# A perceiver block on one core: bias rows turned in 32 by 32 squares, the output bias added later, a longer stretch of written order, and a shorter E4M3 rounding

## The chip, the cores and the metric

The kernel is one launch on one NeuronCore of a Trainium2 chip. Its time is the device time of that core in microseconds (us), from launch to the end of the program. The core's engines each follow their own instruction stream: TensorE (PE in the profile, with its weight loads shown as PEld), VectorE (DVE), ScalarE (ACT), GpSimd (POOL) and SyncE (SP), which here only issues DMAs. They meet through semaphores.

## The reference

Eight batches of 128 rows and 512 features go through three layers; each adds to its input.

```python
x = x + xattn(layernorm(x), ctx, Wq, Wk, Wv, Wo, bo)        # 8 heads of 64, 2048 context rows of 384
x = x + attn(layernorm(x), Wq, bq, Wk, bk, Wv, bv)          # one head of 512, causal mask, softmax over
                                                            # axis 1 of the logits; adds its input twice
x = x + ffn(layernorm(x), w1, b1, w2, b2)                   # 512 -> 2048 -> 512

def ffn(x, w1, b1, w2, b2):
    h  = relu(einsum('bsd,hd->bsh', x, w1) + b1)
    hq = float_quantize(h, 4, 3)      # 4 exponent bits, 3 of mantissa, subnormals, overflow to inf
    wq = float_quantize(w2, 4, 3)
    out = einsum('bsh,dh->bsd', hq, wq) + float_quantize(b2, 5, 10)
    return float_quantize(out, 5, 10)
```

In the second layer the logits are (x Wq + bq)(x Wk + bk)^T. The kernel multiplies Wq and Wk into one matrix and needs the biases only as three small things: bq times bk (one number), Wq times bk (512 numbers, a bias of the keys) and Wk times bq (512 numbers, a row that each x is multiplied with). The key bias is called `side`, the row `u`.

## The kernel before

**Stages.** A head (0 to about 92 us) loads, computes all queries, and the keys and values of batch 0. Then eight batches of cross attention follow. Each has four steps m (two heads each): `scores(b, m)` on TensorE, VectorE reading the eight score banks (L530), ScalarE's exponentials (`exps`, L544), transposes of 32 by 32 squares on VectorE (`turns`, L557), 16 DMAs that move the squares to their places, and one step later `attend` (L571). Between them lie pieces of the next keys and values (`k_proj` L427, `v_proj` L450), which are done by a block product that needs sums of the inputs (`sum_half` L205 for the context, `sum_w` L226 to L239 for the weights). In the last batch these pieces are replaced by the beginning of the self attention of rows 0 to 3: at m = 1 the joint weight (`both_weights`, psw L664), then the four rows' norms (`normed_into` L111 to L118, the product with `u` L649, the bias L652) and their transposes (`turn`, pt_s L131), at m = 2 the keys (psk L678). The feed-forward layer closes (ph L927, pf L936).

**Orders.** TensorE runs in program order throughout. `in_turn` (L241) holds ScalarE and `first` (L243) holds VectorE in program order; both are closed at L859 and L860, in step m = 0 of the last batch. After that, and on POOL and SP everywhere, a scheduler chooses the order from its own estimate of times when the program is built; on the chip each engine then runs strictly in the chosen order.

**The bias rows.** `sa_bk` and `sa_bq` come as 128 columns of 4 numbers. `across` (L284) writes them, 4 bytes at a time, to a line of 512 numbers in DRAM; a second DMA reads that line into all 128 partitions (`row_bk`, `row_bq`, L297). All these DMAs are on POOL's queue. `dot` (L302) multiplies two tiles on VectorE and sums over the row. `dot(both_biases, ...)` and `weight_by_bias(0)` (four dots) stand ahead of `k_proj(0, 0, (1,))` in program order (L783 to L785), `weight_by_bias(1)` behind it. `turn_weight` (L310) transposes squares of Wq and Wk on VectorE; `keep_weights` (L315) writes them out with 32 DMAs on SP.

**The output bias.** `bo` is loaded into all partitions (L276). `keep_rows` (L501) adds it to the eight rows of x on POOL and writes them to DRAM (`xd`) on SP, before `load_q(0)` in program order. `bo`, `row_bk` and `row_bq` share two buffers (tag "t", `TMPB` = 2). The rows `x_in` lie in the buffer that the first transposed exponentials (`pT`) will need.

**Rounding.** `quantize` (L28) rounds with five VectorE instructions: mask the exponent, clamp it, add and subtract a multiple of it (two scalar_tensor_tensor), and scale up and down so that overflow becomes infinite. `quantize_w2` uses it on 16 chunks of w2 (128x512), `hidden` on blocks of four hidden chunks (128x1024; two chunks, 128x512, in the last two blocks), `finish` with the wider format on the result.

Of the kernel before, what the change touches and what calls it, by code (L numbers as in the profile page):

```python
# [17 lines left out]
P = 128  # L18
# [4 lines left out]

E4M3 = (3, -6, 8)
E5M10 = (10, -14, 16)


def quantize(nc, pool, out, x, fmt, tag):  # L28

    man, least, over = fmt
    shape = list(x.shape)
    e = pool.tile(shape, F32, tag=f"{tag}_e", name=f"{tag}_e")
    r = pool.tile(shape, F32, tag=f"{tag}_r", name=f"{tag}_r")
    magic = 1.5 * 2.0 ** (23 - man)
# [4 lines left out]
    nc.vector.tensor_scalar(out, r, 2.0 ** (128 - over), 2.0 ** (over - 128), ALU.mult, ALU.mult)  # L44


@with_exitstack
def tile_perceiver_block(
# [225 lines left out]
    nc.sync.dma_start(wv, xa_wv.rearrange("(k p) n -> p k n", p=P))  # L274
    bo = tmp.tile([P, D], F32, tag="t", name="bo")
    nc.sync.dma_start(bo, xa_bo.partition_broadcast(P))  # L276


    w_sa = vp.tile([P, 2, NK, D], F32, tag="v1", name="w_sa")
    side = const.tile([P, 2, NK], F32, tag="side", name="side")  # L280
# [24 lines left out]
    def weight_by_bias(i):  # L305

        for k in range(NK):
            dot(side[:, i, k : k + 1], w_sa[:, i, k], bias_rows[i])

# [190 lines left out]

    def keep_rows(g):  # L501
        for b in range(g * GB, (g + 1) * GB):
            nc.gpsimd.tensor_tensor(xs[b], xs[b], bo, ALU.add)
        nc.sync.dma_start(xd[:, ts(g, GB), :], x_in[:, ts(g, GB), :])
# [129 lines left out]
    class SelfAttention:  # L634
# [37 lines left out]
        def keys(self, both):  # L672

            self.kt = self.pool.tile([P, NK, GT], F32, tag="sk", name=f"sk_{self.g}")
            for m in range(NK):
                ps = bank(f"psk_{self.g}_{m}")
                for k in range(NK):
                    nc.tensor.matmul(  # L678
                        ps, both[:, k, ts(m, P)], self.xt[:, k, :],
                        start=(k == 0), stop=(k == NK - 1),  # L680
                    )
                nc.scalar.activation(
                    self.kt[:, m, :], ps, AF.Identity, bias=side[:, 0, m : m + 1]
                )
                if m == 1:
                    yield
# [116 lines left out]
    for b in range(B):  # L803
        last = b + 1 == B
        for m in range(NK):
# [45 lines left out]
            if m == 0:  # L851
# [39 lines left out]
    b2r = load_row(wff, b2, "b2r")  # L891
    b1c = load_columns(wff, b1, "b1c")
    w2 = wff.tile([P, NHC, D], BF16, tag="w2", name="w2")
# [17 lines left out]
    def hidden(batches, xt, blocks):  # L911
# [117 lines left out]
```

## Time and profile before

Three runs took 1124.47, 1125.67 and 1127.59 us; the median is 1125.67 us. The profiled execution took 1124.47 us, of which 1122.7 us lie between its first and its last instruction (its span).

| engine | busy us | share of the span | instructions |
|---|---|---|---|
| PE | 1098.4 | 98% | 6254 |
| PEld | 830.2 | 74% | 6254 |
| DVE | 844.1 | 75% | 1760 |
| ACT | 334.7 | 30% | 527 |
| POOL | 236.1 | 21% | 328 |

How to read it: times within the execution count from the span's start. A line of a timeline gives start, duration (of the whole group where it says xN), engine, line of the kernel, operation, output<-input and shapes. A chain line gives start, duration and what ran. In a table of waits, "A <- B: total, times, longest" means that A stood still until B was done. The granted clock is TensorE's clock as the throttle allowed it, 1.00 being full speed.

### The profile page before, as it was taken

How to read it: one execution, taken by the hardware profiler on the slowest of the kernel's cores; microseconds unless marked ns; L12 is line 12 of the kernel's file. 1: busy time of each engine (PE TensorE's matmuls, PEld its weight loads, DVE VectorE, ACT ScalarE, POOL GpSimd, SP SyncE). 2: the span in 40 equal slices, each digit the busy share in tenths (PEclk: the TensorE clock that was granted, in tenths of full speed). 3: DMA queues.
4: the chain of work that ended last, by engine and by line, in shares of the span. 5: the costliest groups of instructions: out<-in, count | busy, mean ns of one | idle time of the engine just before them, and what ended most of it. 6: DMA issues, size and time to landing. Idle time of an engine off the chain costs nothing.

```text
span 1122.7 us, 16820 instructions
## 1 busy us (share of the span) xinstructions
PE 1098.4 (98%) x6254; PEld 830.2 (74%) x6254; DVE 844.1 (75%) x1760; ACT 334.7 (30%) x527; POOL 236.1 (21%) x328
## 2 busy tenths in 40 slices
PE   9989999999999999999999999999998999999997
PEld 4467788877878887888778788878874564687775
DVE  3988767767867786677777667866787468997777
ACT  3323232222223332322222233323232323232221
POOL 1401610440053045004400530350002100000001
PEclk9989999999999999999999999999998999999999
DMA  8858544553553355445535533554474445200001
GB/s 213 279 129 135 129 99 111 146 151 76 142 143 83 85 148 146 101 109 146 150 76 142 141 76 85 148 137 92 108 209 120 108 95 225 75 1 20 10 10 38
DMA packets 66785, 130.10 MB, mean 116 GB/s; under 512 B 27456, under 2 KB 32592, under 8 KB 65808
## 3 DMA queue, kind: packets, MB, share of 16 engines
q1 hardware_dynamic: 64144, 121.68, 43.6%
q0 software_dynamic: 1696, 6.57, 2.0%
q8 instruction: 49, 0.80, 0.3%
q10 hardware_dynamic: 864, 0.79, 0.2%
q14 instruction: 32, 0.26, 0.1%
HBM read 51.92 MB, written 9.97 MB: 55 GB/s over the span
## 4 chain that ended last, share of the span: by engine, by line
PE 88%; DVE 7%; DMA 3%; issue 1%; ACT 0%; SPq 0%; ACTq 0%; DVEq 0%
PE pv_z L450 20%; PE pk_z L427 19%; PE po L571 11%; PE sc L526 10%; PE ph L927 9%; PE pv_b L450 3%; PE pk_b L427 3%; PE psk L678 2%; PE psv L717 2%; PE py L609 2%; PE pf L936 2%; DMA x<-in_ctx_t_dram 1%; PE psw L664 1%; DVE m L205 1%; DMA x_in<-in_x_dram 1%; DVE x L205 1%
## 5 line engine op out<-in xcount | busy, mean ns | idle before, releaser
L544 ACT ACTIVATE p<-p,nm 128x2048 f32<-128x2048 f32 x64 | 128.2, 2003 | 429.4 <-DVE nm L538 291.2
L557 DVE STREAM_TRANSPOSE p<-p 128x512 f32<-128x512 f32 x256 | 158.9, 680 | 82.8 <-ACT p L544 82.6
L530 DVE TENSOR_SCALAR_CACHE_REDUCE p<-sc 128x512 f32<-128x512 f32 x256 | 159.0, 686 | 21.0 <-PE sc L526 18.6
L450 PE MATMUL pv_z<-wv_sums,x 128*128 128x256 f32 x640 | 158.0, 381 | 1.8 <-DVE v L353 1.8
L427 PE MATMUL pk_z<-x,wk_sums 128*128 128x256 f32 x600 | 151.0, 385 | 5.5 <-DVE kt L353 4.9
L205 POOL TENSOR_TENSOR m<-x 128x256 f32<-128x256 f32 x70 | 51.1, 731 | 485.4 <-DMA x<-in_ctx_t_dram 388.9
L450 PEld LDWEIGHTS pv_z<-wv_sums,x 128*128 128x128 f32 x640 | 120.4, 190 | 20.3 <-DVE v L353 2.2
L427 PEld LDWEIGHTS pk_z<-x,wk_sums 128*128 128x128 f32 x600 | 113.4, 191 | 25.1 <-DVE kt L353 5.6
L571 PEld LDWEIGHTS po<-pT,v 128*64 128x64 f32 x2048 | 112.4, 138 | 25.0 <-issue 23.5
L526 PE MATMUL sc<-kt,q 64*128 64x512 f32 x512 | 120.9, 604 | 3.8 <-DVE p L530 2.5
L571 PE MATMUL po<-pT,v 128*64 128x128 f32 x2048 | 120.2, 276 | 0.0
L927 PE MATMUL ph<-xf,w 128*128 128x256 f32 x512 | 111.3, 379 | 0.0
L450 PE MATMUL pv_z<-wv_sums,m 128*128 128x256 f32 x448 | 107.5, 380 | 0.2 <-ACT v L347 0.2
L927 PEld LDWEIGHTS ph<-xf,w 128*128 128x128 f32 x512 | 97.2, 190 | 13.9 <-issue 0.5
L427 PE MATMUL pk_z<-m,wk_sums 128*128 128x256 f32 x420 | 102.0, 381 | 0.0
L526 PEld LDWEIGHTS sc<-kt,q 64*128 64x128 f32 x512 | 47.6, 187 | 63.7 <-issue 52.7
L450 PEld LDWEIGHTS pv_z<-wv_sums,m 128*128 128x128 f32 x448 | 83.3, 190 | 13.3 <-issue 0.9
L427 PEld LDWEIGHTS pk_z<-m,wk_sums 128*128 128x128 f32 x420 | 79.8, 191 | 11.7
L347 ACT COPY v<-pv_z 128x512 f32<-128x512 f32 x112 | 62.8, 588 | 59.8 <-PE pv_z L450 59.6
L347 ACT COPY kt<-pk_z 128x512 f32<-128x512 f32 (+1 forms) x112 | 59.7, 558 | 63.1 <-PE pk_z L427 62.7
L205 POOL TENSOR_TENSOR x<-x 128x256 f32<-128x256 f32 x98 | 69.9, 730 | 0.8 <-DMA x<-in_ctx_t_dram 0.7
L350 DVE TENSOR_TENSOR v<-pv_z,v 128x512 f32<-128x512 f32 x96 | 63.2, 686 | 5.1 <-PE pv_z L450 5.0
(187 smaller groups left out, 1233.1 us busy)
## 6 DMA issues: line engine op xcount, KB each, us to landing
pT<-p SPq DMA_DIRECT2D x512, 128.0 KB, 2.4
x<-in_ctx_t_dram SPq DMA_DIRECT2D x45, 512.0 KB, 5.6
w<-in_w_t_dram SPq DMA_DIRECT2D x1, 4096.0 KB, 12.6
w2f<-in_w_t_dram SPq DMA_DIRECT2D x16, 256.0 KB, 2.7
x_in<-in_x_dram SPq DMA_DIRECT2D x8, 256.0 KB, 13.0
xd<-x_in SPq DMA_DIRECT2D x2, 1024.0 KB, 4.4
qd<-xq SPq DMA_DIRECT2D x8, 256.0 KB, 5.2
q<-qd SPq DMA_DIRECT2D x8, 256.0 KB, 3.1
```

The lines of the kernel that those rows point to most:

```text
L205: eng.tensor_tensor(x_block(b, h, to), x_block(b, h, one), x_block(b, h, two), ALU.add if op == "+" else ALU.subtract,)
L347: nc.scalar.copy(outs[ij], views(ps))
L350: nc.vector.tensor_tensor(outs[to], views(ps), outs[other], op)
L427: nc.tensor.matmul(ps[:, ts(i, BK)], wk_sums[:, WSLOT[WAT[r]], f2, :], x_block(b, h, XAT[r]), start=start and i == 0, stop=True, skip_grou ...
L450: nc.tensor.matmul(ps[:, ts(t, 256)], x[:, ts(t, P)], wv_sums[:, WSLOT[WAT[r]], :], start=start and t == 0, stop=True, skip_group_check=True,)
L526: nc.tensor.matmul(pair[i], q[r, :], kts[b, m // 2][r, m % 2, ts(n, 512)], start=True, stop=True)
L530: nc.vector.tensor_scalar(p[:, :, i].rearrange("p g (t i) -> p t g i", i=SQ)[:, ts(n, Q)], pair[i].rearrange("p (t g i) -> p t g i", g=Q, ...
L544: nc.scalar.activation(p[:, :, i], p[:, :, i], AF.Exp, bias=nms[b, m][:, i : i + 1], scale=SCALE, accum_out=sums[b][:, h : h + 1],)
L557: nc.vector.transpose(p[:, g, i], p[:, g, i])
L571: nc.tensor.matmul(pos[b][h * DH : (h + 1) * DH, ts(m, P)].rearrange("p (a i) -> p a i", a=Q), v[:, jt % 8, ts(2 * m + h, DH)], turned_[b, ...
L609: nc.tensor.matmul(ps, ot[:, ts(k, P)], wo[:, k, :], start=(k == 0), stop=(k == NK - 1))
L927: nc.tensor.matmul(ps[:, :n], w1[:, k, ts(c, P)], xt[:, k, at], start=(k == 0), stop=(k == NK - 1),)
```

## The change

Four edits.

1. **Bias rows by squares.** `sa_bk` and `sa_bq` are now loaded on SP (behind the loads of Wq and Wk) into the first four columns of zeroed 128x32 tiles (`squares`). `across(n)` transposes one such tile on VectorE in squares of 32, so that each band of 32 partitions holds four rows of 32 numbers, and writes them to DRAM with four POOL DMAs of four 128-byte pieces each. `spread_biases()`, called after the two `sum_half` of VectorE and before `sum_w` of the values' weights, does this for both rows and reads them back into all partitions. The third line, `u`, goes the same way behind `weight_by_bias(1)`.
2. **Output bias.** `bo` is allocated and loaded behind `weight_by_bias(0)`, in the buffer that `row_bk` leaves, and `keep_rows` follows it. The whole `turn_weight(0)` moves there too, ahead of `k_proj(0, 0, (1,))`.
3. **Program order.** `first` and `in_turn` are closed at the end of step m = 1 of the last batch, behind the norms and transposes of rows 0 to 3, and no longer at the end of m = 0.
4. **Rounding to E4M3.** `round_e4m3` gets x and a second tile c, which ScalarE makes: |x| (or relu of the same sum) times 2^20 in bfloat16. Subtracting x from c in float32 rounds it to the last place of c, three binary places below the leading one of x. VectorE clamps c, subtracts x from it, subtracts the difference from c, and scales: four instructions, two of them on bfloat16 alone. ScalarE gets one more activation for each chunk. The wider format keeps `quantize`.

```diff
-E4M3 = (3, -6, 8)
...
+UP = 2.0**20
+LOWEST, HIGHEST = 1.5 * 2.0**14, 2.0**30
+INFINITE = 2.0**120
+def round_e4m3(nc, pool, out, x, c, tag):
+    d = pool.tile(list(x.shape), F32, tag=f"{tag}_d", name=f"{tag}_d")
+    nc.vector.tensor_scalar(c, c, LOWEST, HIGHEST, ALU.max, ALU.min)
+    nc.vector.tensor_tensor(d, c, x, ALU.subtract)
+    nc.vector.tensor_tensor(out, c, d, ALU.subtract)
+    nc.vector.tensor_scalar(out, out, INFINITE, 1.0 / INFINITE, ALU.mult, ALU.mult)
...
-    bo = tmp.tile([P, D], F32, tag="t", name="bo")
-    nc.sync.dma_start(bo, xa_bo.partition_broadcast(P))
...
-    def across(v, n, name):
-        line = dram.tile([1, D], F32, tag=f"line{n}", name=f"line_{n}")
-        nc.gpsimd.dma_start(line.rearrange("o (k p) -> p (o k)", p=P), v)
-        return line[0].partition_broadcast(P)
+    squares = const.tile([P, 3, SQ], F32, tag="squares", name="squares")
+    nc.gpsimd.memset(squares, 0.0)
+    def across(n):
+        line = dram.tile([NK, P], F32, tag=f"line{n}", name=f"line_{n}")
+        nc.vector.transpose(squares[:, n], squares[:, n])
+        for a in range(Q):
+            nc.gpsimd.dma_start(line[:, ts(a, SQ)], squares[a * SQ : a * SQ + NK, n])
+        return line.rearrange("k p -> (k p)").partition_broadcast(P)
...
+    for n, a in enumerate((sa_bk, sa_bq)):
+        nc.sync.dma_start(squares[:, n, :NK], a)
     bias_rows = []
-    for n, a in (("bk", sa_bk), ("bq", sa_bq)):
-        c = const.tile([P, NK], F32, tag=f"c{n}", name=f"c_{n}")
-        nc.gpsimd.dma_start(c, a)
-        t = tmp.tile([P, D], F32, tag="t", name=f"row_{n}")
-        nc.gpsimd.dma_start(t, across(c, n, n))
-        bias_rows.append(t)
+    def spread_biases():
+        for n in range(2):
+            t = tmp.tile([P, D], F32, tag="t", name=f"row_{n}")
+            nc.gpsimd.dma_start(t, across(n))
+            bias_rows.append(t)
...
     sum_half(0, 1, nc.vector)
     sum_half(0, 0, nc.vector)
+    spread_biases()
     sum_w(lambda k, j: wv3[:, k, j, :], wv_sums, nc.vector)
     q_proj(1, both[1], qds[1], range(NK))
-    for g in range(NG):
-        keep_rows(g)
     load_q(0)
     dot(both_biases, bias_rows[0], bias_rows[1])
     weight_by_bias(0)
+    bo = tmp.tile([P, D], F32, tag="t", name="bo")
+    nc.sync.dma_start(bo, xa_bo.partition_broadcast(P))
+    for g in range(NG):
+        keep_rows(g)
+    turn_weight(0, range(NK))
     all_of(k_proj(0, 0, (1,)))
     weight_by_bias(1)
-    u_line = across(side[:, 1], "u", "u")
-    turn_weight(0, range(2))
+    u_line = across(2)
     values = first_of(v_proj(0, 0))
     first_of(values)
-    turn_weight(0, range(2, NK))
     turn_weight(1, range(NK))
     keep_weights()
...
                 if last:
-                    first.close()
-                    in_turn.close()
                     sap, w = enter_self_attention()
                     sa0 = SelfAttention(0, sap, w)
             if last and m == 1:
                 for r in sa0.rows:
                     sa0.norm(r)
                     sa0.turn(r)
+                first.close()
+                in_turn.close()
...
-            quantize(nc, tp, w2[:, c, :], w, E4M3, "qb")
+            up = tp.tile([P, D], BF16, tag="w2c", name=f"w2c_{c}")
+            nc.scalar.activation(up, w, AF.Abs, scale=UP)
+            round_e4m3(nc, tp, w2[:, c, :], w, up, "qw")
...
+            up = tp.tile([P, per, n], BF16, tag="hc", name=f"hc_{b0}_{c0}")
...
                 nc.scalar.activation(h[:, i, :], ps[:, :n], AF.Relu, bias=b1c[:, c : c + 1])
-            quantize(nc, tp, firsts[b0][:, c0 : c0 + per, :], h, E4M3, "qh")
+                nc.scalar.activation(
+                    up[:, i, :], ps[:, :n], AF.Relu, bias=b1up[:, c : c + 1], scale=UP
+                )
+            round_e4m3(nc, tp, firsts[b0][:, c0 : c0 + per, :], h, up, "qh")
```

More of the change, by code (lines that the diff above doesn't have):

```diff
@@ L274, in tile_perceiver_block @@
     nc.sync.dma_start(wv, xa_wv.rearrange("(k p) n -> p k n", p=P))
-    bo = tmp.tile([P, D], F32, tag="t", name="bo")
-    nc.sync.dma_start(bo, xa_bo.partition_broadcast(P))
     w_sa = vp.tile([P, 2, NK, D], F32, tag="v1", name="w_sa")
-    side = const.tile([P, 2, NK], F32, tag="side", name="side")
+    side = const.tile([P, NK], F32, tag="side", name="side")
     both_biases = const.tile([P, 1], F32, tag="both_biases", name="both_biases")
     turned_w = [dram.tile([D, D], F32, tag=f"tw{i}", name=f"tw_{i}") for i in range(2)]
-    def across(v, n, name):
-        line = dram.tile([1, D], F32, tag=f"line{n}", name=f"line_{n}")
-        nc.gpsimd.dma_start(line.rearrange("o (k p) -> p (o k)", p=P), v)
-        return line[0].partition_broadcast(P)
+    squares = const.tile([P, 3, SQ], F32, tag="squares", name="squares")
[6 more added lines that the diff above has]
+        return line.rearrange("k p -> (k p)").partition_broadcast(P)
     for i, a in enumerate((sa_wq, sa_wk)):
         nc.sync.dma_start(w_sa[:, i], a.rearrange("(k p) n -> p k n", p=P))
+    for n, a in enumerate((sa_bk, sa_bq)):
+        nc.sync.dma_start(squares[:, n, :NK], a)
     bias_rows = []
-    for n, a in (("bk", sa_bk), ("bq", sa_bq)):
-        c = const.tile([P, NK], F32, tag=f"c{n}", name=f"c_{n}")
-        nc.gpsimd.dma_start(c, a)
-        t = tmp.tile([P, D], F32, tag="t", name=f"row_{n}")
-        nc.gpsimd.dma_start(t, across(c, n, n))
-        bias_rows.append(t)
+    def spread_biases():
[3 more added lines that the diff above has]
+            bias_rows.append(t)
     unread = ps_acc.tile([P, D], F32, tag="po", name="unread")
@@ L307, in weight_by_bias @@
         for k in range(NK):
-            dot(side[:, i, k : k + 1], w_sa[:, i, k], bias_rows[i])
+            to = squares[:, 2] if i else side
+            dot(to[:, k : k + 1], w_sa[:, i, k], bias_rows[i])
     def turn_weight(i, ks):
@@ L682, in keys @@
                 nc.scalar.activation(
-                    self.kt[:, m, :], ps, AF.Identity, bias=side[:, 0, m : m + 1]
+                    self.kt[:, m, :], ps, AF.Identity, bias=side[:, m : m + 1]
                 )
@@ L892, in tile_perceiver_block @@
     b1c = load_columns(wff, b1, "b1c")
+    b1up = wff.tile([P, NHC], F32, tag="b1up", name="b1up")
+    nc.gpsimd.tensor_scalar(b1up, b1c, UP, None, ALU.mult)
     w2 = wff.tile([P, NHC, D], BF16, tag="w2", name="w2")
```

## The prediction

> **What bounds the kernel now.** First the page: TensorE is busy for 98% of the span. A change pays only where TensorE stands still, or where it makes it stand still.
>
> ```profile
> PE 1098.4 (98%) x6254; PEld 830.2 (74%) x6254; DVE 844.1 (75%) x1760; ACT 334.7 (30%) x527; POOL 236.1 (21%) x328
> ```
>
> Second, TensorE's own waits, here those near the edits.
>
> ```profile
> PE pk_z L427 <- DVE kt L353: 4.9, 1, 4.9
> PE sc L526 <- DVE p L530: 2.5, 1, 2.5
> ...
> PE sc L526 <- DVE rows L612: 1.3, 1, 1.3
> ...
> PE pf L936 <- DVE hq L44: 0.5, 1, 0.5
> ```
>
> The 4.9 us lie in the head (62.97 to 67.90), the 2.5 and 1.3 us in the last batch around 850, the 0.5 us near the end.
>
> Third, the timelines of VectorE and POOL in the head. While POOL adds bo (38.16 to 49.6), a sum of 128x256 takes VectorE 1.37 us; before and after, 0.42 (0.36 from start to start).
>
> ```profile
> 38.16 0.42 DVE L205 TENSOR_TENSOR m<-x,m 128x256 f32<-128x256 f32 x1
> 38.62 1.37 DVE L205 TENSOR_TENSOR x<-x 128x256 f32<-128x256 f32 x1
> ...
> 49.78 0.41 DVE L205 TENSOR_TENSOR x<-x,m 128x256 f32<-128x256 f32 x1
> ...
> 63.65 0.69 DVE L303 SCALAR_TENSOR_TENSOR unread<-row_bk,row_bq 128x512 f32<-128x512 f32 x1
> ...
> 67.43 0.41 DVE L353 TENSOR_TENSOR kt<-kt,pk_z 128x256 f32<-128x256 f32 x1
> ```
>
> ```profile
> 38.16 11.41 POOL L503 TENSOR_TENSOR x_in<-x_in,bo 128x512 f32<-128x512 f32 x8 [19.88 <-DVE m L205]
> ```
>
> Fourth, the windows: after each of the two long stops TensorE's granted clock (behind its five engines, before the DMA share) is 0.50 for 6.83 us.
>
> ```profile
> 66.31:73.14 6.83, 5.24 (x12) 4.21 (x13) 4.26 (x12) 0.37 (x1) 0.00 (x0) 0.50 0.35 130
> ...
> 851.38:858.20 6.82, 4.72 (x28) 3.22 (x30) 6.79 (x23) 1.06 (x1) 0.00 (x0) 0.50 0.01 4
> ```
>
> Fifth, the chain in the last batch, where `attend` takes 4.95 us at the halved clock and 3.65 elsewhere, and one VectorE line of a norm that met a POOL addition.
>
> ```profile
> 853.48 2.07 PE sc L526 x2
> 855.55 4.95 PE po L571 x64
> 860.50 13.93 PE psw L664 x32
> 874.43 1.75 PE pt_s L131 x16
> 876.18 3.63 PE sc L526 x16
> ```
>
> ```profile
> 936.44 1.77 DVE L649 SCALAR_TENSOR_TENSOR unread<-xn_s,u 128x512 bf16<-128x512 f32 x1
> ```
>
> **The head (edits 1 and 2).** Moving `keep_rows` away frees eight slowed sums: from 38.62 to 49.78 they take 11.16 us, at 0.36 each they would take 2.9. The sums end at 58.48 - 8.3 = 50.2, `sum_w` (13 instructions, 5.2 us) at about 55.6. POOL loses the old bias DMAs of the first 18 us; they may let the context land up to 1 us earlier, which I leave out.
>
> But the rows now start late. The transposes of 128x32 end at about 50.4 (a 128x512 one takes 0.68). POOL issues a DMA in 0.54 to 0.79 us, so the eight of the two lines take 4.4 to 6.1. How long four pieces of 128 bytes take to land no row shows. The nearest is the write of turned weights (the same 128-byte pieces, SP's queue), 2.1 us; the column load b1c on POOL's queue took 3.2, and the old line of 512 pieces of 4 bytes 9.9. I take 2.1 to 3.2, by the piece size, and keep 9.9 for a rival. The read into 128 partitions: b2r, same form and queue, 3.5 us when all was quiet, row_bq 6.0 under traffic. With both lines ahead of both reads the second line has landed at 54.25 + 2.1 to 3.2 = 56.4 to 57.5 and the second row at 60 to 63.5; with the first read between the lines (POOL would stand behind its wait) at 62 to 67. So the dots start at 60 to 67, middle 63.5, against 63.65 now: the 8.3 us are eaten by the row's way through DRAM. Behind them stand five dots (0.79 each, 3.9) and the four transposes of `turn_weight(0)` (0.61 each, 2.5, new there), then L353, for which TensorE waits. It goes on at 66.7 to 73.8, middle about 70.1 instead of 67.90. Of the extra 2.2 us some returns: the clock is halved until 73.14 anyway, and what starts later spends less in it: 5.2 us at half rate become 3.0. Net +1.5, with ends -2 (rows at 60) and +5.
>
> What is queued behind. `bo` waits on SP for the last dot of `weight_by_bias(0)` (about 67.6), lands 4 to 9 us later (b2r 3.5, bo 8.7), and POOL's eight additions (11.4) lie between 72 and 88. There they slow the four dots of `weight_by_bias(1)`, from 0.79 to about 1.4 each (one per addition), 2.6 us; VectorE has 2.5 us of transposes less in that stretch, and `v_proj` needs its first VectorE result only at its eleventh product, 3 us after it had it. Cost 0. On SP the two writes of xd (waiting for POOL), the two loads behind them and the 32 writes of turned weights (79.15 to 101.6, 0.7 us each) share one queue. If the scheduler puts the first weights ahead of xd, the queue ends near 102 as now; the turned weights leave the buffer that `v_proj(0, 1)` first writes at 107.55. About 5 us of cover; x_in leaves pT's buffer by 96, which is first written at 109. Cost 0. u's line is read only at 843. Nothing else of the head waits.
>
> **The last batch (edit 3).** Gained: L612 and the score readings (L530) no longer stand behind norms. From 845.70 TensorE needs 3.63 (scores) + 3.65 (attend) and starts psw at 852.98, not 860.50: -7.5, of which 1.3 is the clock. psw ends at 866.9.
>
> Lost: the norms now follow the whole step in both orders. ScalarE's order is exp, two psw copies, exp, two psw copies, load of the Sqrt table, then per row square root and copy. The last psw copy ends at 867.45, the table load (1.28) at 868.73; square root 0.29, reciprocal 0.16, normalize 0.54 with their gaps: first row at 869.85. TensorE, which had 1.75 us of transposes here without a wait, now stands. Each further row costs one round on VectorE: product with u 0.69, its sum and bias 0.15, statistics 0.60 and 0.15, square root 0.35, reciprocal 0.2, normalize 0.55: 2.7 us (the row's transpose and copy, 1.2, fit beside the first half). But POOL adds the row to x (1.27 us) just behind each normalize. Of the eight products with u, the one that met this took 1.77. Then a round is 3.75. The fourth row is ready at 869.85 + 3 x 2.7 to 3.75 = 878 to 881.1, the next scores start at 878.5 to 881.6 instead of 876.18: +2.3 to +5.4. In 867 to 881 TensorE works only 0.44 us per round, so I expect the halved clock again, as at 851; if it holds to about 883.9, it takes 2.7 or 1.1 us more. I take the round of 3.75, since the products that took 0.69 had no addition behind them: +5.4 + 1.1, rounded down to +6; ends +2.3 and +8.
>
> The Trainium skill (SBUF — State Buffer, Who interferes with whom) says that any VectorE instruction with two SBUF inputs is blocked for the whole of a GpSimd instruction that reads SBUF. By it the one-column bias addition L652 waits even where the product slips in first, so 3.75 is the only round; by the seven fast products alone it would be 2.7, and the total 3 us lower before the clock. No row shows L652 against an addition.
>
> Later TensorE is continuous until 931, so this shift stays. The norms of rows 4 to 6 are now placed by the scheduler behind 881; if ahead of score readings, up to 4 us more.
>
> **The rounding (edit 4).** Between 974.56 and 1100.65 TensorE is busy throughout (126.09 of 126.09 us in the windows), so fewer VectorE instructions give nothing there, and ScalarE's second activation (0.47 of each 1.73 us) hides too: ScalarE has 1.25 us free per chunk. If a chunk of w2 held ScalarE's queue, seven PSUM banks cover 12 us. Only the tail counts: the last chain of five (0.42, 0.43, 0.69, 0.69, 0.43; ends 1111.03) becomes one activation (0.47, to 1108.52) and four: two bfloat16 ones between 0.2 and 0.43, two of 0.69. End 1110.4 to 1110.8: -0.4, and the result's chain moves with it.
>
> **Sum.** +1.5 + 6 - 0.4 = +7.1 on the profiled execution's 1124.47 us: 1131.6, 5.9 above the median of 1125.67. I say 1131.5.
>
> **The rivals.** *The norms hide (faster).* The last batch keeps its 7.5 us if the rows come faster than TensorE needs them; break-even is a fourth row at 875.6, a round of 1.9 us. For it: the old norms finished unseen. Against: the round's own rows add to 2.7 on two engines in strict order. Full price: 1124.47 + 1.5 - 7.5 - 0.4 = 1118. Chance 0.15.
> *The two parts cancel.* Round of 2.7, full clock, head -2: 1124.47 - 2 + 2.3 - 0.4 = 1124.4; with the head at 0, 1126.4. Chance 0.17.
> *The lines land as slowly as before* (9.9, then a read of 7.5, as u took): second row at 54.25 + 9.9 + 0.5 + 7.5 = 72.2, TensorE at 79.1, +11 instead of +1.5: 1141. For it: the same queue; against: 16 pieces in place of 512. Chance 0.08.
> *SP's queue blocks*: xd ahead of all turned weights; they start at 88, end at 111, and `v_proj(0, 1)` waits 3 to 4 us: 1135. Chance 0.1.
> *My forecast*, 0.5, own range 1128 to 1135.
>
> **Range and chances.** 1119 to 1139 reaches from the hidden norms to a half-slow line; about 0.1 lies beyond each end. A measurement here tells 0.3% (3.4 us) from no change. Slower: forecast 0.5 less 0.03 for its low end, lines 0.08, queue 0.1, together 0.65. Same: the cancelling case and low end less 0.03 that falls below, 0.17. Faster: hidden norms and that 0.03, 0.18.
>
> **What would show it.** Head: sums at 0.36 us apart to 50; L303's first dot led by a wait for row_bq; TensorE's wait for L353 still 4 to 10 us. Last batch: no wait of sc for L612, psw at 853, then a wait of pt_s for xn_s of 9 to 13 us in four pieces and a clock of 0.50 around it. Tail: no wait for the last rounding above 0.2. I am wrong if pt_s hardly waits (the orders don't bind as I read them), or if the rows land before 57, when the head's wait and its halved clock (20 products in 7.13 us that need 4.3) go and give back up to 7.7 us.

## The result and the profile after

Six runs of the changed kernel took 1132.38 to 1134.42 us, median 1134.19; six of the kernel before on the same chip had a median of 1125.84. The ratio is 1.0066 with a 95% interval of [1.0047, 1.0086]: slower, by about 7.4 us (0.7%, clear of the noise). The profiled execution took 1132.38 us, its span is 1130.6. The forecast was 1131.5 in 1119 to 1139, so the number came out well. The terms it was summed from did not: two of them were wrong by 6 to 10 us each, in opposite directions.

Line numbers have moved; the chunk sums are now L225 (before L205), the dots L328 (L303), the wait in the head is for L379 (L353), the score readings are L557 (L530), and of the norms the scaling is L138, the product with u L676, the one-column bias addition L679 and POOL's addition L144.

First, busy time on the page, one line:

```profile
PE 1099.4 (97%) x6250; PEld 830.2 (73%) x6254; DVE 813.5 (72%) x1730; ACT 368.2 (33%) x607; POOL 240.9 (21%) x337
```

VectorE lost 31 us of work and ScalarE gained 34, and the span grew by 7.9 us. Busy sums say nothing here. TensorE's waits do (who waits, for whom, total, times, longest):

```profile
PE pt_s L151 <- DVE xn_s L138: 10.8, 4, 3.2
PE pt_s L151 <- DVE rs_s L137: 3.3, 1, 3.3
PE sc L553 <- DVE p L557: 3.1, 1, 3.1
PE pv_z L476 <- DVE v L379: 1.8, 1, 1.8
...
PE pk_z L453 <- DVE kt L379: 0.4, 1, 0.4
```

The head's wait of 4.9 us is down to 0.4. The wait for the normed rows, 1.8 us in one entry before, is 14.1 us in five; the 1.8 us for rows 4 to 7 are among them, so 12.3 us in four entries are new. The wait of the scores for p was to go, and has grown from 2.5 to 3.1.

Where the time goes shows best when the same marks on TensorE's timeline are laid side by side. The difference is after minus before.

| mark on TensorE | before, us | after, us | difference |
|---|---|---|---|
| scores(0, 0) starts | 92.25 | 84.30 | -7.95 |
| scores(1, 0) starts | 199.28 | 191.74 | -7.54 |
| scores(7, 1) starts | 845.70 | 837.55 | -8.15 |
| psw starts | 860.43 | 850.70 | -9.73 |
| scores(7, 2) starts | 876.11 | 880.82 | +4.71 |
| first ph | 974.40 | 982.40 | +8.0 |
| end of the span | 1122.7 | 1130.6 | +7.9 |

So the head gives 8 us, the seven batches between change next to nothing, the last batch's step m = 1 takes 12.9 back (+4.71 against -8.15), and what follows takes 3.3 more. The clock explains most of those 3.3: scores(7, 2) took 4.71 us instead of 3.70, and the key products of rows 4 to 7, later on, 15.7 instead of 14.0.

**The head after.** The granted clock stays at 1.00, and what moved first is the load rate. Windows of before (the first two lines) and of after (the next two): the stretch, then its length, the busy time of PE, PEld, DVE, ACT and POOL, the granted clock, the DMA share and GB/s.

```profile
10.00:20.00 10.00, 10.00 (x25) 4.49 (x24) 6.82 (x16) 2.80 (x6) 1.29 (x2) 1.00 0.83 172
20.00:30.00 10.00, 10.00 (x36) 5.31 (x35) 3.79 (x13) 4.59 (x8) 0.00 (x0) 1.00 0.98 234
```

```profile
10.00:20.00 10.00, 10.00 (x25) 4.37 (x24) 7.96 (x23) 4.09 (x7) 0.00 (x0) 1.00 1.03 381
20.00:30.00 10.00, 10.00 (x37) 5.41 (x36) 8.88 (x24) 4.59 (x9) 0.00 (x0) 1.00 1.03 385
```

The DMA engines were busy for most of both stretches in the kernel before too (0.83 and 0.98, against 1.03), and moved 0.45 and 0.61 times as much. Wq landed 8.8 us after its issue instead of 19.0, the second half of the context 8.6 instead of 15.2. VectorE's timeline in the head:

```profile
42.26 0.75 DVE L225 TENSOR_TENSOR x<-x 128x256 f32<-128x256 f32 x2
42.93 0.29 DVE L308 STREAM_TRANSPOSE squares<-squares 128x32 f32<-128x32 f32 x2
...
54.95 0.70 DVE L328 SCALAR_TENSOR_TENSOR unread<-row,row 128x512 f32<-128x512 f32 x1 [4.72 <-DMA row<-line]
```

The sums start at 27.5 instead of 34.6 and end at 43.0 instead of 58.5, each at 0.42 us. The rows' way through DRAM (transposes, eight writes, two reads) takes from 43.2 to 54.95, 11.75 us, and VectorE does wait 4.72 us for it; but all of this now happens before TensorE needs it.

**The last batch after.** VectorE's timeline at the first score reading of step (7, 1):

```profile
837.66 0.69 DVE L639 TENSOR_TENSOR rows<-py,rows 128x512 f32<-128x512 f32 x1 [2.74 <-PE py L636]
843.63 0.69 DVE L557 TENSOR_SCALAR_CACHE_REDUCE p<-sc 128x512 f32<-128x512 f32 x1 [5.28 <-DMA pT<-p]
```

SP's timeline, the issue of the 16 transfers of the step before, which must have left the buffer p:

```profile
821.64 14.71 SPq L587 DMA_DIRECT2D pT<-p  x16
```

Nothing of the norms stands in front any more, and the reading still starts 5.28 us late, because p is still being read by the transfers to pT. They land 7.5 us after their issue here (median); the whole kernel's median is 2.4. In the kernel before, the same 16 transfers took 7.1 us, but there the norms stood in front of the reading as well. Then the norms. VectorE's timeline, one round from the scaling of the first row to that of the second:

```profile
867.16 0.55 DVE L138 TENSOR_SCALAR xn_s<-rows,mv_s,rs_s 128x512 f32<-128x512 f32 x1
867.74 0.69 DVE L676 SCALAR_TENSOR_TENSOR unread<-xn_s,u 128x512 bf16<-128x512 f32 x1
868.47 1.09 DVE L679 TENSOR_TENSOR sc<-sc,both_biases 128x1 f32<-128x1 f32 x1
869.49 0.68 DVE L131 BATCH_NORM_STATS2 st_s<-rows 128x6 f32<-128x512 f32 x1
...
870.95 0.55 DVE L138 TENSOR_SCALAR xn_s<-rows,mv_s,rs_s 128x512 f32<-128x512 f32 x1
```

POOL's timeline, the addition of the second row:

```profile
871.58 1.77 POOL L144 TENSOR_TENSOR rows<-rows,xn_s 128x512 f32<-128x512 f32 x1 [2.02 <-DVE xn_s L138]
```

From scaling to scaling is 3.79 us, and the addition of one column takes 1.09 us while POOL adds a row. TensorE and its clock in the same stretch:

```profile
867.85 0.63 PE L151 MATMUL pt_s<-ident,xn_s 128*128 128x128 f32 x4 [3.15 <-DVE xn_s L138]
871.64 1.09 PE L151 MATMUL pt_s<-ident,xn_s 128*128 128x128 f32 x4 [3.16 <-DVE xn_s L138]
875.43 1.09 PE L151 MATMUL pt_s<-ident,xn_s 128*128 128x128 f32 x4 [2.70 <-DVE xn_s L138]
879.80 1.08 PE L151 MATMUL pt_s<-ident,xn_s 128*128 128x128 f32 x4 [3.28 <-DVE rs_s L137]
880.82 3.43 PE L553 MATMUL sc<-kt,q 64*128 64x512 f32 x10
```

```profile
869.20:882.90 13.70, 5.28 (x18) 3.21 (x20) 12.31 (x30) 3.12 (x8) 5.96 (x5) 0.50 0.23 50
```

The four transposes of a row take 0.63 us at full clock and 1.09 at the halved one; the clock stays halved for 13.7 us.

### The profile page after: what moved, and what is told of

Its sections match the earlier page's. It is cut to its first block, busy times and chain, and to the rows that moved or that the text cites. A ratio compares the mean times of both kernels' runs of the same rounds, so it can differ in the third digit from the quotient of the medians.

```text
span 1130.6 us, 16934 instructions
## 1 busy us (share of the span) xinstructions
PE 1099.4 (97%) x6250; PEld 830.2 (73%) x6254; DVE 813.5 (72%) x1730; ACT 368.2 (33%) x607; POOL 240.9 (21%) x337
## 4 chain that ended last, share of the span: by engine, by line
PE 87%; DVE 7%; DMA 3%; SPq 1%; ACT 1%; issue 1%; POOL 0%; DVEq 0%; POOLq 0%
PE pv_z L476 20%; PE pk_z L453 19%; PE po L598 10%; PE ph L961 10%; PE sc L553 9%; PE pv_b L476 3%; PE pk_b L453 3%; PE psv L744 2%; PE pf L973 2%; PE py L636 2%; DMA pT<-p 2%; PE k L435 2%; PE psk L705 1%; PE psw L691 1%; DVE p L557 1%; SPq L587 1%
## 5 line engine op out<-in xcount | busy, mean ns | idle before, releaser
L557 DVE TENSOR_SCALAR_CACHE_REDUCE p<-sc 128x512 f32<-128x512 f32 x256 | 159.2, 686 | 24.0 <-PE sc L553 18.1
L225 POOL TENSOR_TENSOR m<-x 128x256 f32<-128x256 f32 x70 | 51.2, 731 | 481.0 <-DMA x<-in_ctx_t_dram 333.5
L453 PEld LDWEIGHTS pk_z<-m,wk_sums 128*128 128x128 f32 x420 | 79.2, 190 | 11.7 <-DVE kt L376 0.4
L225 POOL TENSOR_TENSOR x<-x 128x256 f32<-128x256 f32 x98 | 70.0, 732 | 0.4 <-DMA x<-in_ctx_t_dram 0.3
```

The lines of the kernel that those rows point to most:

```text
L225: eng.tensor_tensor(x_block(b, h, to), x_block(b, h, one), x_block(b, h, two), ALU.add if op == "+" else ALU.subtract,)
L453: nc.tensor.matmul(ps[:, ts(i, BK)], wk_sums[:, WSLOT[WAT[r]], f2, :], x_block(b, h, XAT[r]), start=start and i == 0, stop=True, skip_grou ...
L557: nc.vector.tensor_scalar(p[:, :, i].rearrange("p g (t i) -> p t g i", i=SQ)[:, ts(n, Q)], pair[i].rearrange("p (t g i) -> p t g i", g=Q, ...
```

## Theories and experiments

The theory after the result had four parts. (a) The order of edit 3 alone makes the loss in the last batch. (b) The head gains because the old lines, written as 512 pieces of 4 bytes, slowed every load beside them, and because POOL's additions no longer lie beside the sums. (c) The 7.5 us that were to be won at scores(7, 1) were not, because the loads of the self attention's weights share the DMA engines with pT. (d) The rounding is hidden. Rivals are named with each run.

### Edit 3 undone, and edit 3 alone

```diff
 (changed kernel, step m = 0 of the last batch)
+                    first.close()
+                    in_turn.close()
                     sap, w = enter_self_attention()
...
                     sa0.turn(r)
-                first.close()
-                in_turn.close()
```

> The changed kernel with the written orders of VectorE and ScalarE closed where they were before (end of step m = 0 of the last batch); the other three edits stay. Theory (the late close is the whole loss: 16.2 us from the end of psw to the next scores where before had 1.75): 12 to 15 us less than the changed kernel, so 1119 to 1122, below before by 4 to 7; the next scores start 1.7 us after psw, and scores(7, 1) stands again for readings held back on VectorE. Rival (the loss is from the rounding or from the scheduler's other choices after the batches): within 3 us of the changed kernel, 1131 to 1137.

Measured: 1118.61 us (1118.09 to 1120.85), ratio to the kernel before 0.9927 [0.9900, 0.9954]. This is faster than both kernels. The second run is the kernel before with the same lines moved the other way.

> The kernel before with the late close alone. Theory: the norms' rounds of 3.8 us behind psw cost 14 to 17 us less 1 to 2 won at scores(7, 1): 1139 to 1142, with a wait of pt_s for xn_s of about 14 us. Rival (the edits need each other, the late close alone is harmless): within 2 us of before.

Measured: 1144.55 us (1140.68 to 1146.27), ratio 1.0154 [1.0124, 1.0184]. TensorE's waits of this kernel:

```profile
PE pt_s L131 <- DVE xn_s L118: 10.8, 4, 3.2
PE pk_z L427 <- DVE kt L353: 6.6, 1, 6.6
PE pt_s L131 <- DVE rs_s L117: 3.3, 1, 3.3
```

This is above the expected 1139 to 1142. From psw to scores(7, 2) it needs 30.13 us, the changed kernel 30.12, the kernel before 15.68, and the kernel without edit 3 again 15.68, here from its TensorE timeline:

```profile
855.24 14.00 PE L691 MATMUL psw<-swq,swk 128*128 128x512 f32 x32
869.08 1.91 PE L151 MATMUL pt_s<-ident,xn_s 128*128 128x128 f32 x16
870.92 3.70 PE L553 MATMUL sc<-kt,q 64*128 64x512 f32 x16
```

So edit 3 alone makes the loss between these two marks, and makes it whole. The profile of the kernel with edit 3 alone is behind that of the kernel before by 2.9 us at scores(7, 1) already; that lies in the head, whose code is the same, with loads of 157 GB/s where the shown execution had 172.

### Two idle lines of 4-byte pieces

The changed kernel with two lines written in the old way, which nothing reads:

```diff
+    for n, a in (("bk", sa_bk), ("bq", sa_bq)):
+        c = const.tile([P, NK], F32, tag=f"c{n}", name=f"c_{n}")
+        nc.gpsimd.dma_start(c, a)
+        idle = dram.tile([1, D], F32, tag=f"idle{n}", name=f"idle_{n}")
+        nc.gpsimd.dma_start(idle.rearrange("o (k p) -> p (o k)", p=P), c)
     bias_rows = []
```

> The changed kernel plus two DMAs on POOL at the start that write the bias columns, in 512 pieces of 4 bytes each, to a DRAM line that nothing reads (and the loads of these columns, 2 KB each). Nothing is left out. Theory (such pieces are what slowed the loads of the head before): the queries' inputs land 3 to 6 us later, the context's second half 7 us later (near 34 instead of 26), the sums end near 50 instead of 43, the rows land near 62, L353 is late again and TensorE stands 5 us with the clock halved behind it: 6 to 9 us more than the changed kernel, 1140 to 1143. Rival (the loads are quicker because row reads and bo were moved away, the pieces cost nothing): the same as the changed kernel within 1.5 us.

Measured: 1138.19 us (1136.87 to 1139.42), ratio 1.0102 [1.0078, 1.0127]; about 4 us behind the changed kernel, less than expected. Up to the first scores the cost is larger: they start at 93.09 instead of 84.30. Windows, then the first dot on VectorE:

```profile
10.00:20.00 10.00, 10.00 (x25) 4.41 (x24) 6.66 (x16) 2.62 (x5) 0.76 (x1) 1.00 0.78 154
20.00:30.00 10.00, 8.88 (x33) 4.48 (x32) 3.45 (x11) 4.59 (x8) 0.00 (x0) 1.00 1.04 217
```

```profile
61.91 0.70 DVE L333 SCALAR_TENSOR_TENSOR unread<-row,row 128x512 f32<-128x512 f32 x1 [4.20 <-DMA row<-line]
```

The two lines carry 4 KB together and take the loads back to 154 GB/s; Wq again needs 20.0 us to land and TensorE waits 5.1 us for L384. That the lines slow the loads is shown by this run. It adds the loads of the two columns (2 KB each) on POOL as well; but the changed kernel has such loads on SP at 20.04, in the stretch with 385 GB/s, and here the two on POOL have landed by 17.3, while the large loads are slow in the next stretch too (217 GB/s), beside the second line. The first scores are then 0.84 us later than in the kernel before: with slow loads the head comes out near the prediction's +1.5. 2.1 us of the 8.8 have come back by scores(0, 1), the rest stays to the end, where the profiled executions are 7.0 us apart (one is the lowest of the changed kernel's six, the other the highest of this kernel's four; hence the 4 us between the medians).

The Trainium skill (DMA: Bandwidth & Descriptors, Specifications) says that a transfer needs 512 bytes for line rate, below which the engine reads, modifies and writes, and (Queues, rings and completion order) that each DMA engine takes turns between queues by packets. That fits with what this run shows, 154 GB/s with the lines and 381 without at a DMA share of 0.78 and 1.03, but no run here tells which of the two it is.

### Edit 4 alone

The kernel before with `round_e4m3` in `quantize_w2` and, in the same way, in `hidden`:

```diff
-            quantize(nc, tp, w2[:, c, :], w, E4M3, "qb")
+            up = tp.tile([P, D], BF16, tag="w2c", name=f"w2c_{c}")
+            nc.scalar.activation(up, w, AF.Abs, scale=UP)
+            round_e4m3(nc, tp, w2[:, c, :], w, up, "qw")
```

> The kernel before with the new rounding alone. Theory: hidden behind TensorE except for the last chain, 0 to 0.6 us less: 1125 to 1126, no difference to be measured; VectorE some 30 us less busy, ScalarE some 35 us more. Rival (ScalarE's additional activations hold back PSUM banks or norms): 2 to 5 us more.

Measured: 1127.6 us (1123.32 to 1131.36), ratio 1.0003 [0.9986, 1.0020], no difference. In the stretch of the hidden layer TensorE is busy throughout, as before (columns as in the windows above):

```profile
977.00:1102.00 125.00, 125.00 (x584) 100.57 (x583) 75.55 (x115) 52.10 (x126) 6.34 (x5) 1.00 0.03 11
```

### Edit 2 alone, and edit 1 alone

The kernel before with `bo`, `keep_rows` and the whole `turn_weight(0)` behind `weight_by_bias(0)`, and the old bias lines:

```diff
-    bo = tmp.tile([P, D], F32, tag="t", name="bo")
-    nc.sync.dma_start(bo, xa_bo.partition_broadcast(P))
...
-    for g in range(NG):
-        keep_rows(g)
...
     weight_by_bias(0)
+    bo = tmp.tile([P, D], F32, tag="t", name="bo")
+    nc.sync.dma_start(bo, xa_bo.partition_broadcast(P))
+    for g in range(NG):
+        keep_rows(g)
+    turn_weight(0, range(NK))
```

> The kernel before with edit 2 alone: bo and its additions come late, the whole of turn_weight(0) stands behind them, the bias rows are spread in the old way by lines of 4-byte pieces. Theory (the head gains 8 us from two things, each enough for most of it: loads that no line of 4-byte pieces slows, and sums that no addition on POOL slows): the loads stay slow (about 172 and 234 GB/s in 10-20 and 20-30 us), the sums start at about 35-37 us as before but end near 50 instead of 58.5, and since the rows have long landed, the dots follow at once, TensorE's wait of 4.9 us and its halved clock go, and scores(0,0) starts at 85 to 87 instead of 92.25: 1118 to 1121 us. Rival (the gain is the load rate alone): scores(0,0) stays at 91 to 93 and the time within 2 us of the kernel before. Second rival (the late additions and SP's longer queue cost what they free): 1126 to 1130.

Measured: 1127.59 us (1124.72 to 1131.18), ratio 1.0018 [1.0003, 1.0033]. The theory was right up to the first scores (85.94, the wait for L351 0.3) and wrong about the end: at scores(0, 2) the kernel is 1.55 us behind the kernel before, and is still 1.53 behind at scores(7, 1). Between lie two waits of TensorE that the kernel before does not have, 2.48 us and 2.88 us:

```profile
105.41 2.08 PE L448 MATMUL pv_z<-wv_sums,m 128*128 128x256 f32 x4 [2.48 <-ACT v L345]
...
127.51 1.12 PE L524 MATMUL sc<-kt,q 64*128 64x512 f32 x2 [2.88 <-DVE p L528]
```

Behind both stands the queue of SP. Here are its timeline and the reading on VectorE that the second wait is for:

```profile
76.38 26.77 SPq L318 DMA_DIRECT2D tw<-w_sa  x30
...
105.40 16.20 SPq L558 DMA_DIRECT2D pT<-p  x16
```

```profile
126.75 0.69 DVE L528 TENSOR_SCALAR_CACHE_REDUCE p<-sc 128x512 f32<-128x512 f32 x1 [5.02 <-DMA x<-in_ctx_t_dram]
```

With `keep_rows` late, the writes of the turned weights start at 76.38 behind xd, and run beside the third line of 4-byte pieces, u's, which POOL issues at 75.92 and which needs 13.0 us. The 30 issues take 26.8 us on SP, in the changed kernel 18.5 (74.72 to 93.2). The first wait follows at once: ScalarE's copy of the values (L345) stands 6.98 us for a write of turned weights, because the values go into the buffer that these still occupy. That is the prediction's rival of a blocked queue on SP, which comes true here and not in the changed kernel. Everything behind the writes on SP is late: context loads at 103.25 instead of 93.27, and pT's issues take 16.2 us beside them, to 121.6. The reading at L528 then waits 5.02 us; the profile names a context load, which it does not use, and what must have left p are those 16 transfers. This is the second rival of this run. That u's line makes the difference between 26.8 and 18.5 is argued from its place in time. Other runs bear it out in part: the kernel before, which has this line too, takes 22.5 us for its 32 issues, and the next run, in which u goes by squares, 17.5.

The other half, edit 1 alone: squares as in the changed kernel, `bo` and `keep_rows` where the kernel before has them.

```diff
+    for n, a in enumerate((sa_bk, sa_bq)):
+        nc.sync.dma_start(squares[:, n, :NK], a)
...
     sum_half(0, 1, nc.vector)
     sum_half(0, 0, nc.vector)
+    spread_biases()
...
-    u_line = across(side[:, 1], "u", "u")
+    u_line = across(2)
```

> The kernel before with edit 1 alone: bias rows by squares, bo early, its additions on POOL where they were. Theory (as above): the loads run at about 380 GB/s and the sums start at 27-28 us, but the eight additions lie beside them again (8 us more), so that the transposes end near 51, the rows land 11.75 us later at 62-63, and scores(0,0) starts at 91 to 93 as in the kernel before: 1123 to 1128 us, no gain without edit 2. Rival (the load rate alone carries the gain): scores(0,0) at 84 to 87 and 1117 to 1121 us. In neither case does the last batch change.

Measured: 1127.24 us (1124.24 to 1128.24), ratio 1.0020 [1.0003, 1.0036], scores(0, 0) at 94.15, even later than expected. Loads run at 375 and 392 GB/s, the sums lie beside POOL's additions (1.4 to 1.5 us each) and end at 51.9, and the dots wait:

```profile
51.89 0.30 DVE L290 STREAM_TRANSPOSE squares<-squares 128x32 f32<-128x32 f32 x2
...
65.46 0.70 DVE L310 SCALAR_TENSOR_TENSOR unread<-row,row 128x512 f32<-128x512 f32 x1 [8.13 <-DMA row<-line]
```

TensorE stands 7.7 us. So neither edit lowers the time alone (edit 2 does bring the first scores forward by 6.3 us, and loses them again by scores(0, 2)), and each takes away what spoils the other: edit 1 frees the loads but starts the rows after the sums, edit 2 makes the sums end early but lengthens SP's queue, beside which the old way of u's line still lies.

### Weight loads behind pT

The changed kernel, with swk, swq and swv loaded by SP, whose queue holds the transfers of pT of step (7, 0) first:

```diff
-            w.insert(0, load_w(wsa, turned_w[i], NK, n, nc.gpsimd))
-        w.append(load_w(wsa, sa_wv, NK, "swv", nc.gpsimd))
+            w.insert(0, load_w(wsa, turned_w[i], NK, n, nc.sync))
+        w.append(load_w(wsa, sa_wv, NK, "swv", nc.sync))
```

> The changed kernel, with the three loads of swk, swq and swv (1 MB each) issued by SP behind the 16 transfers of pT of step (7,0), instead of by POOL ahead of them. Theory (VectorE's wait of 5.28 us for the buffer p is made by these loads, which share the DMA engines with pT): pT lands in 3 to 5 us instead of 7.2, the wait at scores(7,1) falls below 1.5 us, TensorE's 3.13 us wait for p goes, the psw products start about 5 us earlier than 850.7, everything behind moves with them, and the 14 us between psw and scores(7,2) stay: 1127 to 1131 us. Rival (the wait has another cause, such as the 2 MB of rows that still come ahead, or SP's own queue): the wait stays at 4 to 6 us and the time at 1133 to 1136. Second rival (swk or swq now lands too late for the psw products): a wait of TensorE for swk or swq, 1136 or more.

Measured: 1125.94 us (1124.17 to 1126.93), ratio 1.0006 [0.9990, 1.0022], which is 7 us less than the changed kernel by the two ratios. SP's timeline, and behind it VectorE's first reading:

```profile
821.83 10.05 SPq L587 DMA_DIRECT2D pT<-p  x16
```

```profile
838.91 0.69 DVE L557 TENSOR_SCALAR_CACHE_REDUCE p<-sc 128x512 f32<-128x512 f32 x1 [0.36 <-PE sc L553]
```

The wait for p is gone, pT lands in 2.5 us again, the clock stays at 1.00 there, and psw starts 7.27 us after scores(7, 1), where the prediction wanted 7.28. The loss at pt_s stays (10.7 and 3.3 us). So the gain that was promised for edit 3 exists, but in the changed kernel these three loads stood in its place.

### The norms by hand

With the loads as in the last run, the norms of rows 0 to 3 are written into VectorE's program order where it is idle:

```diff
                 if last:
                     sap, w = enter_self_attention()
                     sa0 = SelfAttention(0, sap, w)
+                    sa0.statistics()
                 if b > 0:
                     project(b - 1, ot)
...
                 exps(b, m, 0)
+                if last and m == 1:
+                    exps(b, m, 1)
                 if unit:
                     first_of(unit)
...
+            if last and m == 1:
+                sa0.rest_of_norms()
             turns(b, m)
...
-                    sa0.norm(r)
+                sa0.add_rows()
+                for r in sa0.rows:
                     sa0.turn(r)
...
+        def statistics(self):
+            for i, b in enumerate(rows):
+                nc.vector.bn_stats(st, xs[b])
+                nc.vector.bn_aggr(mv[:, i], st)
+            nc.scalar.activation(sd, mv[:, :, 1], AF.Sqrt, bias=eps)
+            nc.vector.reciprocal(rs, sd)
```

`rest_of_norms` holds the four scalings, the four products with u, and one addition of `both_biases` to all four columns; `add_rows` adds the normed rows to x on VectorE.

> The changed kernel with the loads as in e7, and with the norms of rows 0 to 3 written into program order where VectorE is idle: the statistics of the four rows (with one square root over four columns) ahead of the addition that waits for py, the four scalings, products with u and one bias addition over four columns behind the maxima of scores(7,1), the two exponentials of step (7,1) back to back, and the additions to the rows on VectorE instead of POOL, behind the transposes. Theory (the changed kernel loses 14 us at pt_s only because VectorE reaches the norms behind its work for psw's time): TensorE no longer waits for pt_s, scores(7,2) starts about 1.8 us behind the last psw product, at 862 to 866 instead of 880.8, and with the head's gain the kernel is ahead of both: 1113 to 1119 us. Rival (VectorE is the bound of the last batch in any order, so that what leaves pt_s comes back at the readings of scores(7,1) or (7,2)): 1122 to 1130.

Measured: 1114.55 us (1113.82 to 1116.35), ratio 0.9910 [0.9889, 0.9931], the fastest kernel here. TensorE's timeline:

```profile
843.51 3.71 PE L598 MATMUL po<-pT,v 128*64 128x128 f32 x64
847.15 14.00 PE L726 MATMUL psw<-swq,swk 128*128 128x512 f32 x32
860.99 1.91 PE L151 MATMUL pt_s<-ident,xn_s 128*128 128x128 f32 x16
862.83 3.70 PE L553 MATMUL sc<-kt,q 64*128 64x512 f32 x14
```

scores(7, 2) starts at 862.83, 18 us earlier than in the changed kernel. VectorE is no bound in that batch; it was given its work in an order that suited it badly. The statistics still hold up the first readings by 2.8 us (841.70 against 838.91 in the run before), for which TensorE waits 1.2.

### Without the additions on POOL

```diff
-            self.xn[b] = normed(b, self.pool, "xn", GB, "s", add_to=True)
+            self.xn[b] = normed(b, self.pool, "xn", GB, "s", add_to=b >= GB)
```

> The changed kernel without the four additions of the normed rows to rows 0 to 3 on POOL; this part of the computation is left out (rows 0 to 3 of each item lack the term x + norm(x)). Theory (in each of the four rounds behind the psw products VectorE's one-column bias addition is held for 1.09 us by POOL's addition, against 0.16 us without it): the bias addition takes 0.15 to 0.2 us, a round 2.8 to 2.95 us instead of 3.79, the last two rounds gain as much, and scores(7,2) starts 3 to 4 us earlier than 880.8: 1129 to 1132 us. Rival (the 1.09 us are the addition's own latency behind the product with u, whose sum it takes): the rounds stay at 3.7 to 3.8 and the time at 1133 to 1136.

Measured: 1130.2 us (1127.8 to 1131.93), ratio 1.0040 [1.0020, 1.0060]. VectorE:

```profile
868.53 0.55 DVE L138 TENSOR_SCALAR xn_s<-rows,mv_s,rs_s 128x512 f32<-128x512 f32 x1
869.11 0.69 DVE L676 SCALAR_TENSOR_TENSOR unread<-xn_s,u 128x512 bf16<-128x512 f32 x1
869.85 0.16 DVE L679 TENSOR_TENSOR sc<-sc,both_biases 128x1 f32<-128x1 f32 x1
...
871.39 0.55 DVE L138 TENSOR_SCALAR xn_s<-rows,mv_s,rs_s 128x512 f32<-128x512 f32 x1
```

The one-column addition takes 0.16 us instead of 1.09, the round 2.86 instead of 3.79, and from psw to scores(7, 2) it is 27.3 us instead of 30.1, three times 0.93 less. This execution started its psw 1.4 us later, so scores(7, 2) came only 1.4 us earlier, where 3 to 4 were expected; the round was the right thing to forecast, the mark was not. The row agrees with what the prediction took from the Trainium skill (SBUF — State Buffer, Who interferes with whom): the additions on POOL hold a VectorE instruction with two SBUF inputs even if it reads one column.

### The order undone and the loads behind

The first and the seventh run together:

```diff
+                    first.close()
+                    in_turn.close()
                     sap, w = enter_self_attention()
...
-            w.insert(0, load_w(wsa, turned_w[i], NK, n, nc.gpsimd))
+            w.insert(0, load_w(wsa, turned_w[i], NK, n, nc.sync))
```

> The changed kernel with edit 3 undone (the written order of VectorE and ScalarE ends before the norms, as in the kernel before) and the three weight loads issued by SP behind the transfers of pT. Theory (two separate losses: the order, which e1 takes away, and the loads' collision with pT, which e7 takes away): the wait for the buffer p no longer hides the scheduled norms, so most of them now stand in front of scores(7,1)'s readings, and only part of the 8 us of e7 comes on top of e1: 1113 to 1118 us, with scores(7,2) at 863 to 869. Rival (the two are one loss, since in e1 the norms fill the very time that the loads cost): 1118 to 1121, as e1.

Measured: 1120.02 us (1118.46 to 1121.58), ratio 0.9950 [0.9931, 0.9968], no faster than the first alone; the rival's range. TensorE's waits:

```profile
PE sc L553 <- DVE rows L639: 3.5, 1, 3.5
PE sc L553 <- DVE p L557: 2.9, 1, 2.9
PE pt_s L151 <- DVE xn_s L138: 1.8, 1, 1.8
```

With p free early, the norms that the scheduler places ahead of the readings are what the scores wait for (6.4 us in two entries), one of them itself held 2.0 us by u's load. In the first run, where pT took 7.5 us to land, they filled time that the transfers took anyway. The two losses lie on top of each other, and only an order that also moves the norms takes both away.

## Why the prediction was right in sum and wrong in its terms

| term | forecast | measured | |
|---|---|---|---|
| head | +1.5 (-2 to +5) | -8.0 at the first scores, -8.15 at scores(7, 1) | wrong |
| scores(7, 1) to psw | -7.5 | -1.6 (14.73 to 13.15) | wrong |
| psw to scores(7, 2) | +12.9 (15.68 to 28.6) | +14.4 (15.68 to 30.1) | right |
| after that, the clock | +1.1 | +3.3 | too small |
| tail | -0.4 | -0.5 at VectorE's last instruction, -0.1 at the end of the span | right, then lost in the last write |
| sum | +7.1 | +7.9 | |

The forecast for psw to scores(7, 2) is taken from its own steps: psw's end 866.9, the rows at 3.75 us, the scores at 881.6, with psw at 852.98; its sum was rounded down by 0.5. Of the 3.3 us behind scores(7, 2)'s start, 1.0 is the clock in these scores, as forecast; 1.7 more is the clock in the later key products and 0.5 a wait for pT, and neither was in the sum.

**The head: a term left out.** The step that failed is the sentence that POOL loses the old bias DMAs, which "may let the context land up to 1 us earlier, which I leave out". They let the second half of the context land 6.6 us faster after its issue and Wq 10.2, and the sums start at 27.5 instead of 34.6. From there the steps hold: the sums at full rate, then the row's way through DRAM at 11.75 us where 9.6 to 13.1 were worked out with both lines ahead of both reads. Started 7 us earlier than forecast (the sums end at 43.0, not 50.2), that way is hidden. The prediction named the outcome as what would make it wrong (rows before 57 give back up to 7.7 us); the first dot started at 54.95. It gave that too little weight, although the profile had both halves of the price: loads at 172 GB/s with the DMA engines 83% busy, beside a line that took 9.5 and 11.7 us to land. The idle lines show that this term makes the miss: with slow loads again the head is 0.84 us behind the kernel before, where +1.5 was forecast. The fast loads matter because edit 1 puts the rows' way behind the sums: edit 2 alone, with slow loads and the old rows, reaches the first scores at 85.94, and edit 1 alone, with fast loads and slow sums, at 94.15.

**The 7.5 us at scores(7, 1).** The step that failed is that, with no norms in front, TensorE "starts psw at 852.98". It took the norms for the last thing that the score readings waited for. Under them lay the transfers of pT, slowed by the 3 MB of weights. A stall that goes has something next in line, and it was not looked for on the DMA queues, where the three loads and the 16 transfers are seen side by side. The run with the loads behind pT restores the 7.27 us.

**The rounds.** Right: 3.79 us against 3.75, with the clock halved. The reason was half right. The prediction's price came from a product with u that met the addition (1.77 us); in all three rounds the product slipped in first at 0.69 and the one-column bias addition was held for 1.09 instead. That was the case that the prediction put beside it. The fourth row came 4.4 us after the third, because statistics of two later rows stood in between (three instructions of L131, where the rounds before have one). At that row POOL's addition started first, at 879.73, and the product met it and took 1.71 us, as the prediction had priced it.

**Covers that held.** The additions slowed the dots of `weight_by_bias(1)` to 1.58 us (forecast 1.4), and TensorE waited 0.4 us in all between 62 and 84. SP's queue ended its turned weights at 93.2. The rounding gave nothing in the hidden layer.

**The sum.** The head was 9.6 us better than forecast, the start of psw 5.9 worse, the rest 4.0 worse. A total within 3 us of the measurement was here an accident of two errors.

## What to carry to other kernels

Before pricing a removed stall, look at what else the waiting instruction needs, on the DMA queues too: the wait that remains is set by the next one, and it may be paid by loads that no edit touches. A few kilobytes written in 4-byte pieces can cost more as traffic than as latency, so a removed DMA should be priced by what the loads beside it gain. Work that lies on one engine in a strict order belongs where that engine is idle, and two edits that only pay together have to be measured together.

## What the runs showed that was not expected

- Two lines of 512 pieces of 4 bytes each, 2 KB a line, hold the loads beside them at 154 to 187 GB/s in the stretch 10 to 20 us; five kernels had such lines. The seven without them had 373 to 381 GB/s.
- The stall for a buffer that transfers still read shows in the profile as a wait of the engine that will write it (5.28 us at L557), with SP's issues stretched from 10.05 to 14.71 us.
- An addition of one column of 128 numbers took 1.09 us beside POOL's addition of 128x512, and 0.16 without it; POOL's addition itself took 1.77 us in these rounds and 1.26 at the fourth row.
